# Listing the eight largest of every 512 adjacency columns, and gathering rows of x, beside the second layer's dense products

## The chip, the cores and the metric

The kernel runs on one core of a Trainium2 chip. The metric is the device time of one execution, in microseconds (us). The kernel before takes 2217.0 us, the median of two timed runs.

## The reference

Four graph layers work on the same node features x (4096 nodes by 128 features) and the same adjacency matrix adj (4096 by 4096, float32). About two in a thousand of its entries, and its diagonal, are nonzero. Each layer adds its result to x and normalizes every row.

```python
x = _layernorm(x + _L0_gnn_ref(x, adj, adj, L0_gnn_W, L0_gnn_a), axis=-1)
x = _layernorm(x + _L1_gnn_ref(x, adj, L1_gnn_W0, L1_gnn_b0, L1_gnn_W1, L1_gnn_b1), axis=-1)
x = _layernorm(x + _L2_gnn_ref(x, adj, L2_gnn_weight, L2_gnn_att_src, L2_gnn_att_dst, L2_gnn_bias), axis=-1)
x = _layernorm(x + _L3_gnn_ref(x, adj, L3_gnn_W_self, L3_gnn_W_neigh), axis=-1)
```

The second of them, where the change lies, is a Chebyshev convolution applied twice, with L = adj:

```python
def cheb_conv(x, L, W, b):
    Tx0 = x
    out = Tx0 @ W[0]
    Tx1 = L @ x
    out = out + Tx1 @ W[1]
    for k in range(2, W.shape[0]):
        Tx2 = 2.0 * (L @ Tx1) - Tx0
        out = out + Tx2 @ W[k]
        Tx0, Tx1 = (Tx1, Tx2)
    return out + b
h = jax.nn.elu(cheb_conv(x, L, W0, b0))
h = jax.nn.elu(cheb_conv(h, L, W1, b1))
```

## The kernel before

The adjacency matrix lies in device memory twice, as adj and as its transpose adjT, both cut by the host into blocks. A block of adjT is 512 by 512 and is loaded as one chunk of 1 MB: a tile of 128 partitions with four slices (k = 0 to 3) of 512 columns. The function `chunk` (line 128) takes the next tile of a pool `ld` of five such buffers and issues the load on SyncE's queue. The node features stay on chip, x by rows (32 tiles of 128 rows) and xT transposed.

The second layer needs four products with the adjacency matrix. They are reordered so that each is of a 4096-by-128 operand. The function `propagate` (line 656) makes one of them. Its outer loop runs over eight blocks of 512 output columns (ib); its inner loop runs over eight chunks (c), and each chunk gives four products of a 128x128 stationary operand with a 128x512 slice of the chunk, all summed in one bank of PSUM. At float32 each product is two matmul instructions in the profile, so a chunk is eight and a block 64. When a block is summed, `propagate` yields it and the caller works on it.

The four products are these. Operands in parentheses are the stationary ones.

- First propagation (x): the block is copied by ScalarE to t1T (line 679), transposed by TensorE and copied by VectorE to t1 (line 681). The order of its chunks is `finished`, the order in which the first layer completed the blocks of x, since it begins while the last blocks of x are still being normalized by VectorE (line 151).
- Second propagation (t1): VectorE makes t2T = 2 p - xT (line 686). TensorE multiplies xT, t1T and t2T by the three W0 matrices, for two halves of the hidden size (line 690). The function `elu` follows for each half: a relu on ScalarE (line 651), a minimum on VectorE (652), an exponential on ScalarE (653), and the sum on VectorE into hT (654). TensorE multiplies hT by twice the third W1 matrix (line 695), and VectorE copies the result to v (line 697).
- Third propagation (v): with hT and W1 added into the same sum (line 705), transposed and copied to w (line 711).
- A fourth product (w), at line 1126, runs in a part whose order is written out by hand, where the third layer's attention work starts on VectorE, ScalarE and GpSimd as blocks of x are completed.

Outside that last part the Tile framework orders the instructions of each engine by their readiness in a model of the program, and by program order among those that are ready. Each engine then runs its own list in order on the chip, and waits on semaphores. A buffer of a pool is taken again when all who use it are done, so a load of a chunk waits for every reader of the chunk that was in its buffer.

GpSimd has no work in the second layer. In the third layer it adds a bias to x (line 775) and makes a part of the products of attention weights and adjacency (lines 891, 892, 897 and 898).

Of the kernel before, what the change touches and what calls it, by code (L numbers as in the profile page):

```python
# [11 lines left out]
F32 = mybir.dt.float32  # L12
BF16 = mybir.dt.bfloat16
I32 = mybir.dt.int32
# [5 lines left out]
P = 128  # L20
IB = 512
TB = IB // P
# [11 lines left out]
def adj_resnorm_d4(ctx: ExitStack, tc: tile.TileContext, x_in, xT_in, adj, adjT, w0g, w0gT, a0, w1a, b1a,  # L34
# [7 lines left out]
    nc = tc.nc  # L42
    N, F = x_in.shape
    NT = N // P
    NB = N // IB
# [15 lines left out]
    x = state.tile([P, NT, F], F32, name="x")  # L61
# [63 lines left out]
    def chunk(pool, src, ib, c, name="chunk", pinned=False):  # L125

        t = pool.tile([P, TB, IB], F32, name=name)
        r = nc.sync.dma_start(t, src[ib, c])
        if pinned:
            tc.keep_in_program_order(r)  # L130
        return t

    def transpose4(pool, name, src, order=lambda r: r):

        p = pool.tile([P, TB, P], F32, name=name)
        for k in range(TB):
            order(nc.tensor.transpose(p[:, k, :], src(k), ident))  # L137
        return p
# [486 lines left out]
    def network(usual):  # L625

        with ExitStack() as whole:
# [3 lines left out]
            with ExitStack() as first, ExitStack() as l1h_pool:  # L631
                ps_acc, ps_tr, ps_mm = [first.enter_context(tc.tile_pool(name=n, bufs=2, space=PSUM, reuse_waits="tile"))
                                        for n in ("ps_acc", "ps_tr", "ps_mm")]
                if not usual:
                    layer0_general(ps_acc, ps_tr, ps_mm)
                    finished = list(range(NB))
                ld = enter(name="ld", bufs=5)
                if usual:
                    finished = layer0(ld, ps_acc, ps_tr, ps_mm)
                dv = state.tile([96, N], BF16, name="dv")  # L640
                l1w = l1h_pool.enter_context(tc.tile_pool(name="l1w", bufs=2, reuse_waits="tile"))
                l1h = l1h_pool.enter_context(tc.tile_pool(name="l1h", bufs=1, reuse_waits="tile"))
                W1A = l1h.tile([P, 3, HID], F32, name="W1A")
                nc.scalar.dma_start(W1A, w1a.rearrange("k p f -> p k f"))
                W1B = l1h.tile([P, 3 * HH, F], F32, name="W1B")
                nc.scalar.dma_start(W1B, w1b.rearrange("k (h p) f -> p (k h) f", p=P))

                def elu(dst, p, bias):
                    r = l1w.tile([P, IB], F32, name="elu_r")
                    n = l1w.tile([P, IB], F32, name="elu_n")  # L650
                    nc.scalar.activation(r, p, AF.Relu, bias=bias)
                    nc.vector.tensor_scalar(n, p, bias, 0.0, op0=ALU.add, op1=ALU.min)
                    nc.scalar.activation(n, n, AF.Exp)
                    nc.vector.scalar_tensor_tensor(dst, n, -1.0, r, op0=ALU.add, op1=ALU.add)

                def propagate(stationary, order=range(NB), beside=None):


                    for ib in range(NB):
                        p = ps_acc.tile([P, IB], F32, name="pacc")  # L660
                        for n, c in enumerate(order):
                            a = chunk(ld, adjT, ib, c)
                            for k in range(TB):
                                nc.tensor.matmul(p, stationary(c * TB + k), a[:, k, :], start=n == 0 and k == 0,  # L664
                                                 stop=n == NB - 1 and k == TB - 1)
                            if beside and n == 0:
                                beside(p, ib)
                        yield ib, slice(ib * IB, (ib + 1) * IB), p

                t1 = state.tile([P, NT, F], F32, name="t1", tag="yn")  # L670
                t1T = l1h.tile([P, N], F32, name="t1T")
                hT = l1h.tile([P, HH, N], F32, name="hT")
                wd = l1h.tile([P, HH, F], F32, name="wd")
                nc.vector.tensor_sub(wd, W1B[:, 0:HH, :], W1B[:, 2 * HH:3 * HH, :])
                w2x = l1h.tile([P, HH, F], F32, name="w2x")
                nc.vector.tensor_scalar_mul(w2x, W1B[:, 2 * HH:3 * HH, :], 2.0)

                for ib, blk, p in propagate(lambda jt: x[:, jt, :], finished):
                    nc.scalar.copy(t1T[:, blk], p)
                    q = transpose4(ps_tr, "ptr", lambda k: t1T[:, (ib * TB + k) * P:(ib * TB + k + 1) * P])  # L680
                    nc.vector.tensor_copy(t1[:, ib * TB:(ib + 1) * TB, :], q)

                v = state.tile([P, NT, F], F32, name="v")
                for ib, blk, p in propagate(lambda jt: t1[:, jt, :]):
                    t2T = l1w.tile([P, IB], F32, name="t2T")
                    nc.vector.scalar_tensor_tensor(t2T, p, 2.0, xT[:, blk], op0=ALU.mult, op1=ALU.subtract)
                    for hh in range(HH):
                        ph = ps_mm.tile([P, IB], F32, name="pmm")
                        for k, r in enumerate((xT[:, blk], t1T[:, blk], t2T)):
                            nc.tensor.matmul(ph, W1A[:, k, hh * P:(hh + 1) * P], r, start=k == 0, stop=k == 2)  # L690
                        elu(hT[:, hh, blk], ph, B1A[:, hh:hh + 1])
                    q = ps_tr.tile([P, TB, F], F32, name="ptr")
                    for k in range(TB):
                        for hh in range(HH):
                            nc.tensor.matmul(q[:, k, :], hT[:, hh, (ib * TB + k) * P:(ib * TB + k + 1) * P],
                                             w2x[:, hh, :], start=hh == 0, stop=hh == HH - 1)
                    nc.vector.tensor_copy(v[:, ib * TB:(ib + 1) * TB, :], q)


                w = state.tile([P, NT, F], F32, name="w", tag="yn")  # L700
                h0T = xT

                def times_w1(p, ib):
                    for hh in range(HH):
                        nc.tensor.matmul(p, W1B[:, HH + hh, :], hT[:, hh, ib * IB:(ib + 1) * IB], start=False, stop=False)

                for ib, blk, p in propagate(lambda jt: v[:, jt, :], beside=times_w1):
                    lvT = l1w.tile([P, IB], F32, name="t2T")
                    nc.scalar.copy(lvT, p)
                    q = transpose4(ps_tr, "ptr", lambda k: lvT[:, k * P:(k + 1) * P])  # L710
                    nc.vector.tensor_copy(w[:, ib * TB:(ib + 1) * TB, :], q)  # L711
                    ph = ps_mm.tile([P, IB], F32, name="pmm")
                    for hh in range(HH):
                        nc.tensor.matmul(ph, wd[:, hh, :], hT[:, hh, blk], start=hh == 0, stop=hh == HH - 1)
                    nc.scalar.copy(h0T[:, blk], ph)
# [328 lines left out]
            with tc.manual_schedule(engines={mybir.EngineType.PE, mybir.EngineType.DVE, mybir.EngineType.Activation,  # L1044
# [68 lines left out]
                for ib in range(NB):  # L1113
                    early = ib == 1
                    p = ps_nd.tile([P, IB], F32, name="num") if early else ps_p.tile([P, IB], F32, name="pp")
                    cuts = [0, 2, 4, 6, 8] if ib < 4 else [0, 1, 2, 4, 5, 6, 8] if ib < 6 else [0, 2, 4, 5, 6, 8]
                    for first, last in zip(cuts, cuts[1:]):
                        ks = [(c, k) for c in range(first, last) for k in range(TB)]
                        for n, (c, k) in enumerate(ks):
# [4 lines left out]
                            if k == 0:  # L1124
                                a = chunk(ld, adjT, ib, c)
# [55 lines left out]
            for _ in layer3_product(this.blocks):  # L1181
                pass

    network(True)
    with tc.If(nc.values_load(flag[0:1, 0:1], min_val=0, max_val=P) != 0):
        network(False)
# [32 lines left out]
```

## Time and profile before

| What | Value |
|---|---|
| Median of the two timed runs | 2217.0 us (2216.08 and 2217.92) |
| Span of the profiled execution, first to last instruction | 2213.3 us |
| TensorE matmul busy | 2139.9 us, 97% |
| VectorE busy | 1186.3 us, 54% |
| ScalarE busy | 562.4 us, 25% |
| GpSimd busy | 857.6 us, 39% |
| DMA moved | 528.18 MB, mean 239 GB/s |
| Granted TensorE clock, mean | 0.991 |

The profiled execution has no time of its own outside its span; the span stands 3.7 us below the median of the timed runs, and sums that are made from the profile are brought to the metric by that amount. PE is TensorE, PEld its load of stationary operands, DVE is VectorE, ACT is ScalarE, POOL is GpSimd, SP is SyncE, and a q behind a name is the engine's queue. The page cuts the span into 40 equal slices of 55 us each; a digit is the busy share in tenths. A line such as "L664 PE MATMUL pacc<-chunk,x" names the line of the kernel, the engine, the operation, the tile written and the tiles read. In a timeline the first number is the start in us, the second the time taken in us; what stands in brackets is the engine's idle time before and what ended it. In the list of waits the three numbers are total us, how often, and the longest.

### The profile page before, as it was taken

Reading aid. Unit: us, or ns where it says so; the run is one execution under the profiler, and the core shown is the slowest. Engines: PE = TensorE matmul, PEld = TensorE weight load, DVE = VectorE, ACT = ScalarE, POOL = GpSimd, SP = SyncE. Lnnn points to the kernel's source line nnn. Section 1 sums busy time; section 2 is a strip of 40 time slices with the busy share of each in tenths; the row PEclk is TensorE's granted clock in tenths of the full one; section 3 lists DMA queues with packets and bytes.
Section 4 is the critical chain, followed back from the end, with each engine's and each line's share of the span. In section 5 each row is a group of like instructions: output and inputs, shape, how many; then the busy total and the mean of one; then the engine's idle time right before and its main releaser. Section 6 shows DMA issues by size and latency. Waiting matters only on the chain. (4 is left out here: it accounts for less than half of the span.)

```text
span 2213.3 us, 22997 instructions
## 1 busy us (share of the span) xinstructions
PE 2139.9 (97%) x8644; PEld 850.8 (38%) x8644; DVE 1186.3 (54%) x1832; ACT 562.4 (25%) x1014; POOL 857.6 (39%) x539
## 2 busy tenths in 40 slices
PE   8999999999999999999999999979999899989997
PEld 3444454444444444444443333322222222333333
DVE  5655460000010110000026877899999999999995
ACT  6755100000000000000043223245333433332213
POOL 0000000000000000000004766698999999999980
PEclk9999999999999999999999999999999999999999
DMA  9886658888767677778876556525666566635545
GB/s 395 334 326 226 228 195 287 300 299 302 265 229 266 230 242 266 262 261 274 283 251 241 195 203 232 209 77 180 247 239 238 183 249 244 228 121 202 191 166 179
DMA packets 87145, 528.18 MB, mean 239 GB/s; under 512 B 9328, under 2 KB 15472, under 8 KB 25712
## 3 DMA queue, kind: packets, MB, share of 16 engines
q1 hardware_dynamic: 80288, 521.64, 66.8%
q10 hardware_dynamic: 6736, 4.98, 0.7%
q8 instruction: 70, 1.15, 0.2%
q14 instruction: 51, 0.42, 0.1%
HBM read 524.49 MB, written 2.10 MB: 238 GB/s over the span
## 5 line engine op out<-in xcount | busy, mean ns | idle before, releaser
L884 DVE SCALAR_TENSOR_TENSOR tau<-D,es,a 128x1024 f32<-128x1024 f32 (+1 forms) x640 | 646.4, 1058 | 44.0 <-ACT a L856 24.8
L892 POOL TENSOR_TENSOR tau<-tau,chunk 128x1024 f32<-128x1024 f32 x192 | 459.2, 2392 | 12.6 <-DVE tau L884 11.7
L775 POOL TENSOR_TENSOR x<-x,B2R 128x512 f32<-128x512 f32 x8 | 10.2, 1276 | 1145.5 <-PE px L137 1145.5
L908 PE MATMUL num<-tau,hc 128*32 128x512 f32 x2048 | 333.9, 606 | 15.0 <-POOL tau L892 9.0
L908 PE MATMUL den<-tau,cs 128*32 128x512 f32 x2048 | 343.6, 597 | 3.3 <-DVE tau L884 0.8
L999 PE MATMUL pp<-chunk,xT 128*128 128x512 f32 (+1 forms) x488 | 232.9, 607 | 0.0
L856 ACT ACTIVATE a<-chunk 128x1024 f32<-128x1024 f32 x160 | 164.2, 1026 | 254.8 <-DVE tau L890 195.1
L664 PE MATMUL pacc<-chunk,t 128*128 128x512 f32 x512 | 223.5, 592 | 0.0
L664 PE MATMUL pacc<-chunk,v 128*128 128x512 f32 x512 | 222.5, 592 | 0.0
L664 PE MATMUL pacc<-chunk,x 128*128 128x512 f32 x512 | 222.1, 592 | 0.0
L891 POOL TENSOR_TENSOR tau<-tau,chunk 128x320 f32<-128x320 f32 x192 | 167.7, 873 | 120.4 <-DVE tau L884 86.5
L1126 PE MATMUL pp<-chunk,w 128*128 128x512 f32 x448 | 204.3, 598 | 0.8 <-DVE oT L749 0.8
L379 PE MATMUL pacc<-chunk,hw 128*128 128x512 f32 x408 | 188.2, 606 | 2.4 <-DVE numT L407 1.7
L890 DVE TENSOR_TENSOR tau<-tau,a 128x704 f32<-128x704 f32 x186 | 163.1, 877 | 0.0
L898 POOL TENSOR_TENSOR tau<-tau,chunk 128x1024 f32<-128x1024 f32 x64 | 151.8, 2372 | 1.0
L908 PEld LDWEIGHTS num<-tau,hc 128*32 128x32 f32 x2048 | 62.4, 109 | 230.9 <-issue 127.8
L908 PEld LDWEIGHTS den<-tau,cs 128*32 128x32 f32 x2048 | 80.4, 110 | 177.0 <-issue 86.9
L664 PEld LDWEIGHTS pacc<-chunk,v 128*128 128x128 f32 x512 | 97.2, 190 | 122.0 <-issue 122.0
L664 PEld LDWEIGHTS pacc<-chunk,x 128*128 128x128 f32 x512 | 96.3, 190 | 115.8 <-issue 115.8
L664 PEld LDWEIGHTS pacc<-chunk,t 128*128 128x128 f32 x512 | 96.1, 190 | 115.3 <-issue 115.3
L999 PEld LDWEIGHTS pp<-chunk,xT 128*128 128x128 f32 x488 | 85.8, 190 | 133.1 <-issue 130.5
L711 DVE COPY w<-ptr 128x512 f32<-128x512 f32 x8 | 5.5, 691 | 241.5 <-PE ptr L137 241.5
(243 smaller groups left out, 1688.6 us busy)
## 6 DMA issues: line engine op xcount, KB each, us to landing
chunk<-in_adjT SPq DMA_DIRECT2D x386, 1024.0 KB, 4.9
chunk<-in_adj SPq DMA_DIRECT2D x80, 1024.0 KB, 5.0
chunk<-in_adj SPq DMA_DIRECT2D x32, 512.0 KB, 4.7
keep<-in_adjT SPq DMA_DIRECT2D x13, 1024.0 KB, 10.0
xT<-in_xT ACTq DMA_DIRECT2D x8, 256.0 KB, 6.6
out<-o ACTq DMA_DIRECT2D x7, 256.0 KB, 2.3
W1A<-in_w1a ACTq DMA_DIRECT2D x1, 384.0 KB, 5.4
W1B<-in_w1b ACTq DMA_DIRECT2D x1, 384.0 KB, 7.4
```

The source lines that it names most:

```text
L379: in_order(nc.tensor.matmul(p, hw[:, j * TB + k, :], a[:, k, :], start=first and k == 0, stop=last and k == TB - 1))
L664: nc.tensor.matmul(p, stationary(c * TB + k), a[:, k, :], start=n == 0 and k == 0, stop=n == NB - 1 and k == TB - 1)
L775: nc.gpsimd.tensor_tensor(x[:, tb, :], x[:, tb, :], B2R[:, None, :].to_broadcast([P, TB, F]), ALU.add)
L856: nc.scalar.activation(ap, a, AF.Copy, accum_out=deg[:, nt, self.mp:self.mp + 1])
L884: nc.vector.scalar_tensor_tensor(flat(tau[:, q:q + n]), flat(self.D[:, q:q + n]), es[:, nt, head:head + 1], ap, op0=ALU.max, op1=ALU.mult)
L890: nc.vector.tensor_tensor(t2[:, 0:OWN], t[:, 0:OWN], (a if only else ap)[:, 0:OWN], ALU.mult)
L891: nc.gpsimd.tensor_tensor(t2[:, OWN:WB], t[:, OWN:WB], a[:, OWN:WB], ALU.mult)
L892: nc.gpsimd.tensor_tensor(t2[:, WB:2 * WB], t[:, WB:2 * WB], a, ALU.mult)
L898: nc.gpsimd.tensor_tensor(tau2[:, 2:4, :], tau[:, 2:4, :], rep(a, 2), ALU.mult)
L908: nc.tensor.matmul(acc[32 * q:32 * q + 32, :], weights(nt, head, is_den), r[:, q, :], start=nt == 0, stop=nt == NT - 1)
L999: nc.tensor.matmul(p, y[:, c * TB + k, :], a[:, k, lo:lo + n], start=c == blocks[0] and k == 0, stop=end)
L1126: nc.tensor.matmul(p, w[:, c * TB + k, :], a[:, k, :], start=c == 0 and k == 0, stop=c == NB - 1 and k == TB - 1)
```

## The change

Each call of `propagate` can be given a function `seen`, which is called with every chunk. In the first propagation VectorE lists the chunks with an even c, in the second those with an odd c: for each of the four 128x512 slices of the chunk, the eight largest elements of each partition's 512 go to the tile `top`, and their positions to the tile `at`. Over both propagations every chunk is listed once. Nothing reads `top` or `at` later.

A table of 4096 rows in device memory receives a copy of x, by one DMA on ScalarE's queue. Then GpSimd issues 16 indirect DMAs for each of the eight blocks of the first propagation; each fetches 128 rows of 512 bytes from the table, one for each partition, by indices that stand in a column of the tile `rows`. They go to a tile `got` of four times 128 columns, of which there are two in turn. The indices are fixed numbers from a pattern (31 times the partition, plus the column), and nothing reads `got`. So the computation of the kernel's output is the same as before, dense products included.

```diff
-                def propagate(stationary, order=range(NB), beside=None):
+                def propagate(stationary, order=range(NB), beside=None, seen=None):
 
 
                     for ib in range(NB):
                         p = ps_acc.tile([P, IB], F32, name="pacc")
                         for n, c in enumerate(order):
                             a = chunk(ld, adjT, ib, c)
+                            if seen:
+                                seen(ib, c, a)
                             for k in range(TB):
                                 nc.tensor.matmul(p, stationary(c * TB + k), a[:, k, :], start=n == 0 and k == 0,
                                                  stop=n == NB - 1 and k == TB - 1)
...
-                for ib, blk, p in propagate(lambda jt: x[:, jt, :], finished):
+                if usual:
+                    top = l1h.tile([P, NT, NB, 8], F32, name="top")
+                    at = l1h.tile([P, NT, NB, 8], mybir.dt.uint16, name="at")
+                    rows = l1h.tile([P, 32], I32, name="rows")
+                    nc.gpsimd.iota(rows, pattern=[[1, 32]], base=0, channel_multiplier=31)
+                    table = whole.enter_context(tc.tile_pool(name="table", bufs=1, space=bass.MemoryType.DRAM)).tile([N, F], F32, name="table")
+                    nc.scalar.dma_start(table.rearrange("(t p) f -> p t f", p=P), x)
+
+                def largest(parity):
+                    def seen(ib, c, a):
+                        if c % 2 == parity:
+                            for k in range(TB):
+                                nc.vector.max(top[:, c * TB + k, ib, :], a[:, k, :])
+                                nc.vector.max_index(at[:, c * TB + k, ib, :], top[:, c * TB + k, ib, :], a[:, k, :])
+                    return seen if usual else None
+
+                for ib, blk, p in propagate(lambda jt: x[:, jt, :], finished, seen=largest(0)):
+                    if usual:
+                        for g in range(4):
+                            got = l1w.tile([P, 4, F], F32, name="got")
+                            for k in range(4):
+                                n = (ib * 16 + g * 4 + k) % 32
+                                nc.gpsimd.indirect_dma_start(got[:, k, :], None, table, bass.IndirectOffsetOnAxis(ap=rows[:, n:n + 1], axis=0))
                     nc.scalar.copy(t1T[:, blk], p)
                     q = transpose4(ps_tr, "ptr", lambda k: t1T[:, (ib * TB + k) * P:(ib * TB + k + 1) * P])
                     nc.vector.tensor_copy(t1[:, ib * TB:(ib + 1) * TB, :], q)
 
                 v = state.tile([P, NT, F], F32, name="v")
-                for ib, blk, p in propagate(lambda jt: t1[:, jt, :]):
+                for ib, blk, p in propagate(lambda jt: t1[:, jt, :], seen=largest(1)):
                     t2T = l1w.tile([P, IB], F32, name="t2T")
```

## The prediction

> **What bounds the kernel now.** I read the page first, for the span and for who is idle where. Slices 7 to 19 of its busy rows are the second layer: PE is at 9 throughout, VectorE at 0 or 1, GpSimd at 0.
>
> ```profile
> PE   8999999999999999999999999979999899989997
> DVE  5655460000010110000026877899999999999995
> POOL 0000000000000000000004766698999999999980
> PEclk9999999999999999999999999999999999999999
> DMA  9886658888767677778876556525666566635545
> ```
>
> Then I cut this part by the three propagations, by the first and last start of their matmuls (324.1 to 551.1 on x, 551.5 to 819.9 on t1, 825.5 to 1075.9 on v). The table of windows shows what room there is beside TensorE:
>
> ```profile
> core 0: us, PE busy (x) PEld busy (x) DVE busy (x) ACT busy (x) POOL busy (x), PEclk, DMA share, GB/s
> 337.00:551.00 214.00, 214.00 (x520) 95.45 (x519) 4.84 (x7) 4.10 (x7) 0.00 (x0) 1.00 0.88 300
> 551.00:825.00 274.00, 274.00 (x725) 128.32 (x724) 31.95 (x45) 21.29 (x32) 0.00 (x0) 1.00 0.73 251
> ```
>
> TensorE sets the pace in both: no idle, full clock. VectorE has 209 us free in the first and 242 us in the second. GpSimd is empty, and its timeline has nothing between 1.3 us and 1115.66 us:
>
> ```profile
> 1.01 0.29 POOL masks.py:199 TENSOR_SCALAR_AFFINE_SELECT ident<-ident 128x128 f32<-128x128 f32 x1
> 1115.66 1.27 POOL L775 TENSOR_TENSOR x<-x,B2R 128x512 f32<-128x512 f32 x1 [1114.36 <-PE px L137]
> ```
>
> Third, VectorE's timeline in the second propagation, which shows the only VectorE operations there for which TensorE waits soon:
>
> ```profile
> 614.08 0.69 DVE L686 SCALAR_TENSOR_TENSOR t2T<-pacc,xT 128x512 f32<-128x512 f32 x1 [22.49 <-PE pacc L664]
> 617.44 0.75 DVE L652 TENSOR_SCALAR elu_n<-pmm,B1A 128x512 f32<-128x512 f32 x1 [2.66 <-ACT elu_r L651]
> 618.88 0.69 DVE L654 SCALAR_TENSOR_TENSOR hT<-elu_n,elu_r 128x512 f32<-128x512 f32 x1 [0.70 <-ACT elu_n L653]
> ```
>
> Last, the waits of SyncE's queue, which issues the loads, and the landing of the chunk loads from 337 to 551 us: a load waits for TensorE to give back one of five buffers, and then lands quickly.
>
> ```profile
> SPq L128 <- PE pacc L664: 670.4, 191, 8.4
> ```
>
> ```profile
> DMA to landing us min/median/max: 4.6/4.8/5.7
> ```
>
> **The pace and the slack of a chunk.** In the first propagation blocks end every 27.94 us (the t1T copies stand at 384.08, 412.03, 439.97), so a chunk is used every 3.49 us, or 3.43 us of matmuls. A load starts when the chunk five before it is released, and TensorE begins on its data four chunks later, 13.7 us; it lands after 4.8 us. So a chunk lies ready about 8.9 us before it is needed, and VectorE may hold a buffer up to 8.9 us beyond TensorE before anything waits. In the second propagation blocks take 34.41 us (t2T at 579.68, 614.08, 648.49).
>
> [...]
>
> **The change part by part.** Nothing is removed, and none of the results is read later. So it can only cost; the question is what is hidden.
>
> *Listing.* The first propagation lists even chunks, the second odd ones: 8 blocks x 4 chunks x 4 tiles = 128 tiles in each. One tile: the maxima 0.69 us (nearest row, 128x512 f32), loading the eight values 0.16 us (128x4 operations of this trace take 0.16), a hand-over 0.04 us (dependent 128x4 operations follow at 0.20), the search 0.69 us, less 0.08 us in which independent operations overlap (300.48 to 301.06 for one of 0.66). That is 1.50 us. Lower bound 1.2 (two passes at 0.60, no load), upper 2.03[...]. Per block 16 x 1.50 = 24.0 us, plus 0.7 in the first propagation = 24.7 of 27.94, and plus 4.3 (0.69, twice 0.75 and 0.69, 0.69) in the second = 28.3 of 34.41. VectorE keeps up. Even chunks that follow each other in the order of the first propagation let it fall behind for a few us, which the 8.9 us cover. Cost: 0. If that cover were gone, each us above 27.94 per block would show on TensorE.
>
> *What queues behind a listing.* VectorE runs in order. At a block's end in the first propagation only the copy of t1 waits, needed one propagation later: 0. In the second, t2T is ready 0.83 us before TensorE takes it (ends 580.37, used 581.20), and hT 0.74 us before (584.92 + 0.69 = 585.61, used 586.35). One listing operation in front, 0.69, just fits; two do not, and ScalarE's and VectorE's steps alternate. Bounds 0 and 3 us a block; I take 0.8: 8 x 0.8 = 6 us. Before 335 us VectorE also finishes layer 0, with TensorE behind it in order; listing operations in its gaps cost 0 to 6 us, I take 2.
>
> *The table.* ScalarE's queue issues one DMA of x, 4096 rows of 512 B, once x is done at 335.4 us. The next thing due from ScalarE after its copies of xT is t1T at 356.14, so a block on its queue of under 1 us (the like-shaped load of x took 0.84 us to issue, 13.0 us to land) is hidden. A 512 B packet takes 27 ns and an 8192 B packet 309 ns in the packets of this trace, so the table holds each of 16 engines for 256 x 27 ns = 6.9 us.
>
> *The gathers.* 128 DMAs of 128 rows: 8 rows per engine each, 1024 x 27 ns = 27.6 us per engine in all. They wait only for the table, the index tile and a buffer, not for the block. A chunk takes an engine 8 x 309 ns = 2.47 us, so the first propagation needs 64 x 2.47 = 158 us; with 6.9 and 27.6 it is 193 of about 228. The busy share 0.88 is higher than this since one packet in ten takes over 0.6 us; but between 150 and 160 us the same queue ran at 419 GB/s, against 300 needed. Cost 0, by 8.9 us of early landing. GpSimd's own time per gather is in no row.[...] I take 2: 256 us, done near 600 us, long before 1115.66. Cost: 0.
>
> Sum: 2213.3 + 6 + 2 = 2221.3 us of span. The span lies 3.7 us under the median of the two timed runs, 2217.0; so 2225.
>
> **Rivals.**
> 1. *VectorE becomes the bound, slower.* At 2.03 us a tile the first propagation needs 32.5 + 0.7 = 33.2 us a block, 5.3 above TensorE's, 42 us in eight, less 9 of buffers = 33. The second needs 36.8 against 34.41, 19 us, and some 8 us as its chain finds VectorE always busy. With the 2 above, 62: 2279. It passes 2% (44 us) from about 1.97 us a tile. For it: the search has no row, and two passes leave 14% of VectorE in the first propagation.[...]
> 2. *GpSimd is late, slower.* The first product of the third layer that needs it starts at 1176.24; from 337 us that allows (1176 - 337) / 128 = 6.6 us a gather.[...] at 7 us about 2280. For it: unmeasured, one index a partition.[...]
> 3. *The loads starve.* If a gathered row took 200 ns instead of 27, the engines would owe 128 x 2.47 + 205 + 7 = 528 us in the 496 us of both propagations: 32 us, with the chain's 8 about 2257. Against: the 512 B packets of this trace.
> 4. *The listings are dropped or fully hidden*: 2217. Nothing reads them, but nothing in the code takes them out.
>
> **How the numbers follow.** Forecast 0.58, rival 1 0.18, rival 2 0.12, rival 3 0.07, rival 4 0.05. A change within 2%, 44 us, is about what a measurement of this kernel can tell from none. Slower by more takes rivals 1 and 2 and a part of 3 and of the forecast's upper end: 0.36. Faster by over 2% has no mechanism, as nothing is removed: 0.01. Within: 0.63. The range runs from 2215 (all hidden, spread of the timed runs) to 2285 (rival 1 entire, rival 2 up to 7 us); it leaves out most of rival 2 and little else. The likeliest case alone: 2216 to 2236.
>
> **What would show it.** Right: blocks of the first propagation still end every 27.9 us; each listing instruction near 0.69 us; VectorE near 0.87 busy at 337 to 551; GpSimd's last gather before 700 us; TensorE's new idle time in the second propagation put down to t2T or hT. Wrong: chunk loads that wait for VectorE's search and not for TensorE, blocks longer than 28 us (rival 1); line 775 or 891 starting after 1180 (rival 2); landings over 9 us and matmuls that wait for chunk loads (rival 3).

## Result, and the profile after

The changed kernel took 2349.7 us (two runs, 2348.4 and 2351.1) against 2217.0: a ratio of 1.0605, 95% interval 1.0574 to 1.0636. It is slower by 6%. The profiled execution took 2351.06 us, with a span of 2349.0.

That is not the whole result. Run again on four chips, this same kernel took 2216.0 us (12 runs), 2215.8 (10 runs) and 2218.1 (one run) on three of them, and 2348.2 (one run) on the fourth. So the experiments have two questions: what takes the 133 us where they are lost, and why only there.

The busy rows of the page after, each digit a slice of 58.7 us, show where the time went:

```profile
PE   8999998317999999999999999997999999989997
DVE  5654685105776767100002577789999999999995
POOL 0000005770000000000000466669999999999990
PEclk9999999558999999999999999999999999999999
DMA  9886666336886766787777655653666566635445
```

TensorE was at 9 throughout before. Now it falls to 8, 3, 1 and 7 in slices 6 to 9, counted from 0, and GpSimd, empty there before, is at 5, 7 and 7 in slices 6 to 8. DMA falls to 3 in slices 7 and 8: the transfers were not crowded, they were missing. The list of TensorE's instructions on the accumulator gives the three propagations (first and last start):

```profile
L666 PE MATMUL pacc<-chunk,x x512: 589/592/1222, 323.6 to 685.2; 128*128 128x512 f32 x171
L666 PE MATMUL pacc<-chunk,t x512: 592/592/595, 685.7 to 955.5; 128*128 128x512 f32 x171
L666 PE MATMUL pacc<-chunk,v x512: 592/592/595, 961.1 to 1211.8; 128*128 128x512 f32 x171
```

From the first matmul on x to the first on t it is 362.1 us, before 227.4: 134.7 more. From there to the first on v it is 275.4 us, before 274.0. So 134.7 of the 135.7 us by which the span grew lie in the first propagation. The table of windows, cut there by what GpSimd does (gathers from 364.0 to 523.6 us):

```profile
core 0: us, PE busy (x) PEld busy (x) DVE busy (x) ACT busy (x) POOL busy (x), PEclk, DMA share, GB/s
324.00:365.00 41.00, 40.17 (x114) 18.66 (x113) 33.40 (x105) 2.94 (x6) 0.97 (x1) 1.00 0.88 316
365.00:410.00 45.00, 38.22 (x85) 16.77 (x84) 23.15 (x55) 0.58 (x1) 33.20 (x37) 0.92 0.61 212
410.00:525.00 115.00, 28.09 (x28) 7.38 (x27) 15.35 (x36) 0.00 (x0) 86.77 (x92) 0.51 0.34 99
525.00:560.00 35.00, 15.89 (x34) 7.49 (x35) 10.92 (x25) 0.58 (x1) 0.00 (x0) 0.65 0.48 167
560.00:700.00 140.00, 140.00 (x342) 62.47 (x341) 104.85 (x245) 2.93 (x5) 0.00 (x0) 1.00 0.87 301
```

TensorE has its full pace up to the gathers, starts 28 matmuls in 115 us while they run, and has its full pace again soon after. The new groups of the page (count, busy us, mean ns, idle time before and what ended it):

```profile
L702 POOL DMA_INDIRECT got<-table,rows x128 | 120.9, 945 | 402.1 <-DVE top L692 362.6
L692 DVE MAX8 top<-chunk 128x8 f32<-128x512 f32 x256 | 163.3, 679 | 155.8 <-DMA chunk<-in_adjT 116.0
L693 DVE FIND_INDEX8 at<-top,chunk 128x8 uint16<-128x512 f32 x256 | 172.1, 684 | 0.0
```

Each pass of the listing has the length that was forecast. VectorE waits for loads. The other way round it is rare: SyncE's queue waits three times for VectorE's search, 11.0 us in all, each time before 365 us, where TensorE stays busy, and never during the stall. TensorE's timeline during the gathers (start, length, and in brackets the idle time before it with its releaser):

```profile
444.00 1.01 PE L666 MATMUL pacc<-chunk,x 128*128 128x512 f32 x1 [2.36 <-issue]
446.80 1.01 PE L666 MATMUL pacc<-chunk,x 128*128 128x512 f32 x1 [1.79 <-issue]
...
484.60 2.08 PE L666 MATMUL pacc<-chunk,x 128*128 128x512 f32 x2 [3.18 <-DMA chunk<-in_adjT]
544.11 1.11 PE L137 MATMUL ptr<-ident,t1T 128*128 128x128 f32 x4 [57.43 <-ACT t1T L703]
```

The matmuls of a chunk start 2.1 to 4.2 us apart, six of the eight alone and two together, and most gaps are put to "issue", that is to nothing the profile shows. Chunks come about 22.4 us apart, 8 x 2.8. The last two lines show a second effect: the block's last matmul ends at 486.68, and the copy of t1T that waits for it starts at 543.47 (ScalarE's timeline), 56.8 us later, with ScalarE idle all the time. In the kernel before, the 64 matmuls of a block took 27.63 us, one every 0.43 us, and the copy started within a microsecond of their end; the two lines of before stand last here:

```profile
543.47 0.58 ACT L703 COPY t1T<-pacc 128x512 f32<-128x512 f32 x1 [153.53 <-remote]
```

```profile
413.16 27.63 PE L664 MATMUL pacc<-chunk,x 128*128 128x512 f32 x64
439.97 0.59 ACT L679 COPY t1T<-pacc 128x512 f32<-128x512 f32 x1 [27.36 <-PE pacc L664]
```

So TensorE's instructions run late and its completions are seen late, and both stop about 20 us after the gathers do. The granted clock of 0.51 goes with it, but does not make the gaps: a matmul of 1.01 us in place of 0.59 explains 0.4 us of 2.8, and from 365 to 390 us TensorE already stands idle for 5.8 us at a clock of 0.98.

### The profile page after: what moved, and what is told of

Its sections match the earlier page's. It is cut to its first block, busy times and chain, and to the rows that moved or that the text cites. A ratio compares the mean times of both kernels' runs of the same rounds, so it can differ in the third digit from the quotient of the medians.

```text
span 2349.0 us, 23964 instructions
## 1 busy us (share of the span) xinstructions
PE 2163.6 (92%) x8644; PEld 855.7 (36%) x8644; DVE 1508.1 (64%) x2600; ACT 561.7 (24%) x1014; POOL 978.7 (42%) x668
## 3 DMA queue, kind: packets, MB, share of 16 engines
q0 software_dynamic: 4096, 8.40, 1.3%
## 5 line engine op out<-in xcount | busy, mean ns | idle before, releaser
L908 DVE SCALAR_TENSOR_TENSOR tau<-D,es,a 128x1024 f32<-128x1024 f32 (+1 forms) x640 | 646.4, 1058 | 43.0 <-ACT a L880 24.5
L666 PE MATMUL pacc<-chunk,x 128*128 128x512 f32 x512 | 243.0, 627 | 49.5 <-issue 41.3
L702 POOL DMA_INDIRECT got<-table,rows x128 | 120.9, 945 | 402.1 <-DVE top L692 362.6
L692 DVE MAX8 top<-chunk 128x8 f32<-128x512 f32 x256 | 163.3, 679 | 155.8 <-DMA chunk<-in_adjT 116.0
L693 DVE FIND_INDEX8 at<-top,chunk 128x8 uint16<-128x512 f32 x256 | 172.1, 684 | 0.0
```

The source lines that it names most:

```text
L693: nc.vector.max_index(at[:, c * TB + k, ib, :], top[:, c * TB + k, ib, :], a[:, k, :])
L908: nc.vector.scalar_tensor_tensor(flat(tau[:, q:q + n]), flat(self.D[:, q:q + n]), es[:, nt, head:head + 1], ap, op0=ALU.max, op1=ALU.mult)
```

## Experiments

The numbers of chips only tell them apart; the chip of the two recorded runs is not known. "Kernel before" is the median beside it on the same chip. A time that has no count of runs beside it is one run.

### One half of the change alone, and other ways to issue the transfers (chip 1, kernel before 2213.8)

Listing alone:

```
-  rows = ...; nc.gpsimd.iota(rows, ...); table = ...; nc.scalar.dma_start(table, x)
-  nc.gpsimd.indirect_dma_start(got[:, k, :], None, table, ...)        # 128 of them
```

> The table and the 128 gathers are left out, the listing stays. Theory A (the stall from 390 to 540 us comes with the gathers; the listing is hidden): about 2219 us, that is before plus the 2 us by which the second and third propagation grew in the changed kernel, and the first propagation ends near 551 us as before. Theory B (the listing holds the chunk buffers and so starves TensorE): about 2340 us, the first propagation again near 685 us.

Measured: 2215.15 us (20 runs), ratio 1.0006, interval 0.9999 to 1.0012. The listing is hidden on this chip.

Gathers alone:

```
-  top = ...; at = ...
-  return seen if usual else None
+  return None
```

> The listing is left out, the table and the 128 gathers stay. Theory A: the stall is there with its whole size, about 2347 us, loads of chunks again 22.4 us apart while the gathers run. Theory B: about 2217 us. If the two only together make the stall (both readers of a chunk and the gathers), about 2217 us here and about 2219 us with the listing alone.

Measured: 2214.2. During the gathers a load still starts every 3.49 us (46 between 366.1 and 523.0 us), at 350 GB/s. I read this as "the gathers are not enough", and the experiments that followed built on it. That was wrong, as shown below.

Plain transfers of 128 rows, issued by GpSimd or by ScalarE:

```
-  nc.gpsimd.indirect_dma_start(got[:, k, :], None, table, bass.IndirectOffsetOnAxis(ap=rows[:, n:n + 1], axis=0))
+  nc.gpsimd.dma_start(got[:, k, :], table[n * P:(n + 1) * P, :])      # or nc.scalar.dma_start
```

> Listing and table stay; the 128 indirect gathers become 128 plain copies of 128 rows of the table, issued by GpSimd too, same bytes, same rows of 512 B, no indices. Theory A1[...]: a stall again, 2320 to 2350 us, while GpSimd issues. Theory A2 (the indirect form does it[...]): about 2219 us.

> As the one before, but ScalarE's queue issues the 128 plain copies. Theory A1[...]: no stall of 22 us a chunk, about 2219 us, up to 2230 where ScalarE's copies of t1T wait behind the issues. Theory A3 (the traffic of 16,384 rows of 512 B itself, whoever issues it): 2300 us or more.

Measured: 2215.9 from GpSimd and 2263.3 from ScalarE. The second loses 49 us in an ordinary way. On ScalarE's timeline the first three t1T copies stand behind transfers: they start at 371.24 us after 20 of them, at 413.54 after 75, and at 457.75 after all 128. Issuing these holds ScalarE's queue for 0.45 us each (median), 58 us in all, and in between the queue waits for a free `got` buffer: they take from 358.3 to 457.3 us. From the waits of TensorE in that kernel (total us, times, longest):

```profile
PE ptr L137 <- ACT t1T L701: 40.7, 3, 14.9
```

GpSimd waits for the same buffers, but no work for which TensorE waits stands behind it. Its list of instructions on `got` in the kernel with plain transfers from GpSimd, with the waits ahead of them:

```profile
L700 POOL DMA_DIRECT2D got<-table x128: 534/534/707, 364.5 to 498.6; - x128
...
  DMA got<-table: 64.3, 27
```

### Variants of what seemed to be an interaction (chip 13, kernel before 2214.5)

Two GpSimd additions on a scratch tile after each gather, all of them kept in the order of the program:

```
+  for _ in range(2):
+      nc.gpsimd.tensor_tensor(pad, pad, pad, ALU.add)
```

> Listing, table and gathers all stay; GpSimd adds a scratch tile to itself twice after each gather, some 2.5 us, so that a gather starts every 3.8 us and not every 1.25 us. Theory C1 (TensorE's completions pile up only while gathers come close together beside the listing): the stall is gone, 2215 to 2225 us. Theory C2 (each gather beside the listing costs TensorE about 1 us, 135 us for 128): the cost stays, 2340 us, spread over the first two propagations.

A quarter of each row gathered:

```
-  got[:, k, :], None, table
+  got[:, k, 0:32], None, table.rearrange("n (q f) -> (n q) f", q=4)
```

> As the changed kernel, but each gathered row is 128 bytes and not 512:[...] a quarter of the bytes. If the descriptors or the indirect instruction do it: 2350 us as with whole rows. If the bytes written into the on-chip memory do it: well below, 2215 to 2260 us.

Two plain reductions in place of the listing:

```
-  nc.vector.max(...); nc.vector.max_index(...)
+  nc.vector.tensor_reduce(top[...], a[:, k, :], AX.X, ALU.max); nc.vector.tensor_reduce(..., ALU.add)
```

> Gathers and table stay. In place of the eight largest and their positions VectorE makes the maximum and the sum of each 128x512 slice: two passes of about 0.69 us over the same chunks at the same places, but no pair of dependent instructions. Theory D1 (any VectorE work of this density beside indirect gathers does it): 2340 to 2350 us. Theory D2 (it is particular to the listing instructions, with their short load and the semaphore between): about 2217 us.

The listing reads xT and not the chunk:

```
-  nc.vector.max(top[...], a[:, k, :])                # and max_index
+  nc.vector.max(top[...], xT[:, c * IB:(c + 1) * IB])
```

> Gathers and table stay; the listing instructions are as many, but read columns of xT and not the chunk, so that they neither hold a chunk's buffer nor add VectorE to what a load of a chunk waits for. If the stall comes from chunks held by two readers: about 2217 us. If it comes from the listing instructions running beside the gathers, whatever they read: 2330 us or more.

Measured: 2227.1, 2215.7, 2215.8 and 2231.8, none with a stall in the first propagation. Since the unedited kernel was not among them, they say nothing on what the stall needs. Two of them, the additions and the listing on xT, cost time for reasons that can be read. With xT, the listing needs no load and keeps VectorE busy without a gap from 365 to 560 us and beyond (its first instruction starts at 319.5, its last at 665.4); the first t2T of the second propagation queues behind it. From TensorE's waits:

```profile
PE pmm L714 <- DVE t2T L710: 13.9, 1, 13.9
```

With the additions, the loss (288.0 us for 274.0) lies in the second propagation. From the groups of VectorE and of GpSimd there:

```profile
L654 DVE SCALAR_TENSOR_TENSOR hT<-elu_n,elu_r 128x512 f32<-128x512 f32 x14 | 22.4, 1603 | 0.7 <-ACT elu_n L653 0.7
...
L714 DVE SCALAR_TENSOR_TENSOR t2T<-pacc,xT 128x512 f32<-128x512 f32 x7 | 4.8, 688 | 1.2 <-PE pacc L666 1.0
...
L706 POOL TENSOR_TENSOR pad<-pad 128x512 f32<-128x512 f32 x256 | 270.8, 1058 | 12.2
```

The same operation that makes hT takes 675 ns in the changed kernel without the additions (on chip 9). Beside GpSimd's additions it takes 1603 ns, and TensorE waits 11.1 us for it, most of the 14.0. The operation that makes t2T, with one operand in PSUM, keeps its 688 ns. The trace does not say why one slows and the other does not.

### The kernel again, and three more variants (chip 9, kernel before 2214.0)

The changed kernel, nothing edited:

> The changed kernel once more, nothing edited, on whatever chip this call gets. Theory together (search instructions on chunk and whole-row gathers, 1.25 us apart, hold back TensorE's completions): the first propagation is as long as before, about 361 us, the kernel at 2345 to 2355 in every round. Rival chance (the stall is a matter of that chip or of how two streams happened to fall together, so that the near variants which kept 2214 to 2231 say nothing on their edits): the rounds scatter between 2217 and 2350, or all lie near 2217.

Measured: 2216.0 us (12 runs, 2213.9 to 2217.0), ratio 1.0009, interval 1.0000 to 1.0018. No stall in any run. The profile of one of them, windows and gathers:

```profile
410.00:525.00 115.00, 115.00 (x283) 51.39 (x283) 84.38 (x197) 2.93 (x5) 81.40 (x87) 1.00 0.98 349
```

```profile
L702 POOL DMA_INDIRECT got<-table,rows x128: 938/944/1129, 362.6 to 530.0; - x128
...
DMA to landing us min/median/max: 3.3/5.4/6.7
```

The instructions are the same, the gathers run at nearly the same time and take the same 944 ns each, but TensorE has no gap, and 349 GB/s are moved in that window instead of 99. The theory that listing and gathers hold TensorE back wherever they overlap fell here, and with it every reading of the variants above as a cure.

The gathers written at the block ends of the third propagation, where nothing is listed:

```
   for ib, blk, p in propagate(lambda jt: v[:, jt, :], beside=times_w1):
+      (the 16 gathers of the block)
```

> All of the change's work, but the 16 gathers of a block are issued at the block ends of the third propagation, where nothing is listed, instead of the first. Theory together: listing and gathers no longer overlap, no stall, 2214 to 2219 as with the listing alone. Rival gathers with chunk loads (the gathers hold back any propagation that runs close to its loads): the stall moves to the third propagation, its 250 us become about 385, the kernel near 2350. In both the gathers stay 1.25 us apart.

Measured: 2215.8 (20 runs), but the edit did not do what it was for. The gathers still stood from 362.4 to 526.3 us, beside the listing:

```profile
L731 POOL DMA_INDIRECT got<-table,rows x128: 938/944/1129, 362.4 to 526.3; - x128
```

GpSimd's queue holds nothing else there, and a gather waits for no block, so where it is written in the loop does not set when it is issued.

No positions (`max_index` left out), and half of the matmuls of the first propagation (`range(0, TB, 2)`), which leaves out half of its sum:

> The positions are left out: VectorE finds the eight largest (MAX8) and looks up no index; the gathers stay. If the look-up (MATCH_VALUE_LOAD with FIND_INDEX8) is the part of the listing that meets the gathers: no stall, 2214 to 2219. If any search instruction that reads chunk does, or if VectorE's reading of chunk alone does: half as many instructions, a stall of half the size or all of it, 2280 to 2350.

> The first propagation multiplies only the even 128-row tiles of each 512-row chunk (2 matmuls a chunk for 4; half of the sum is left out); loads, listing and gathers stay. Outside the gathers the loads bound it at about 3.0 us a chunk or less. If the stall has a price for each TensorE instruction that signals (22.4 us a chunk over four matmuls with their weight loads), chunks come 11 us apart while the gathers run, and the first propagation lasts some 225 to 300 us. If it has a price for each chunk load or each listed tile, 22 us as before and about 340 to 360 us. If the stall needs a full TensorE queue, it is gone, and the first propagation takes about 200 us.

Measured: 2218.8 and 2179.0, no stall in either, which on this chip tells nothing of the stall. The second has the loads as its bound: the first propagation takes 193.9 us, 3.0 us a chunk, at 399 GB/s between 410 and 525 us.

### On which chips, and is the listing needed

The rest were repeats of two kernels: the changed kernel and the gathers alone. First on chip 4 (kernel before 2213.6):

> The changed kernel again, nothing edited. Theory chip (the stall belongs to the chip, or the session, of the recorded run): 2214 to 2218 here in every round, unless this call gets such a chip, and then about 2350 in every round. Theory chance (it comes and goes from run to run): some rounds near 2217, some near 2350.

> Gathers without the listing, on the chip of the run beside it. If the changed kernel stalls on this chip: 2214 here says that listing and gathers are needed together, 2350 that the gathers are enough. If it does not stall there: 2214 to 2217, and nothing told.

Measured: 2215.8 (10 runs, 2214.5 to 2219.3; ratio 1.0010, interval 1.0000 to 1.0020) and 2215.5. No stall.

The changed kernel on chip 7 and on chip 5:

> The changed kernel, nothing edited, one look on a chip not used for it yet. Theory chip or session (of the recorded run alone): 2214 to 2218. If stalling chips are common, about 2350.

> The changed kernel, nothing edited, one more look. Theory chip or session (of the recorded run alone): 2214 to 2218. If stalling chips are common, about 2350.

Measured: 2218.1 on chip 7 (kernel before 2214.1), 2348.2 on chip 5 (kernel before 2216.4). The windows of these two, chip 7 ahead:

```profile
410.00:525.00 115.00, 115.00 (x284) 51.60 (x283) 84.08 (x197) 2.93 (x5) 79.59 (x85) 1.00 0.97 349
```

```profile
410.00:525.00 115.00, 31.32 (x32) 8.50 (x31) 16.30 (x39) 0.00 (x0) 84.94 (x91) 0.51 0.33 98
```

The stall came back in the size of the recorded runs (first propagation 360.8 us, there 362.1). The kernel before ran at its usual time on this chip.

The gathers alone, on chip 9 and on chip 0:

> Gathers without the listing. On the chip where the changed kernel takes 2348: if the gathers alone hold TensorE's completions back, about 2348 again; if the listing is needed beside them, 2214 to 2218. On any other chip 2214 to 2218, which tells nothing new.

> Gathers without the listing once more. On the chip where the changed kernel takes 2348: about 2348 if the gathers alone are enough, 2214 to 2218 if the listing is needed beside them. On any other chip 2214 to 2218, which tells nothing new.

Measured: 2214.6 on chip 9 (kernel before 2214.5), and 2341.6 on chip 0 (kernel before 2213.6). On chip 0, the first propagation and the gathers, from the lists of instructions:

```profile
L666 PE MATMUL pacc<-chunk,x x512: 589/592/1222, 322.7 to 676.7; 128*128 128x512 f32 x171
```

```profile
L700 POOL DMA_INDIRECT got<-table,rows x128: 939/946/1131, 355.9 to 516.1; - x128
```

TensorE's timeline has the same two signs, with VectorE almost empty (0.69 us busy in the 115 us from 410 to 525):

```profile
440.50 1.01 PE L666 MATMUL pacc<-chunk,x 128*128 128x512 f32 x1 [1.58 <-issue]
443.30 1.01 PE L666 MATMUL pacc<-chunk,x 128*128 128x512 f32 x1 [1.79 <-issue]
...
506.10 2.08 PE L666 MATMUL pacc<-chunk,x 128*128 128x512 f32 x2 [2.90 <-DMA chunk<-in_adjT]
536.61 1.12 PE L137 MATMUL ptr<-ident,t1T 128*128 128x128 f32 x4 [28.43 <-ACT t1T L701]
```

The first propagation lasts 354.4 us (322.7 to the first matmul on t1 at 677.1) with gathers and no listing at all; before it is 227.4. That answers the first question: the listing is not needed, and the table with its indirect gathers is enough, on a chip that stalls. It costs 128.0 us there, against 131.8 with the listing on chip 5 and 132.7 in the recorded runs. Whether the listing adds the few us between them was not measured on one chip, and the listing alone was not run where the stall occurs.

It also tells something of the earlier chips. The gathers alone did not stall on chip 1, and two of the kernels of chip 13 kept all 128 gathers unchanged and did not stall. So neither chip was one that stalled at the time, and none of the variants run there can have cured anything.

**What is shown, and what stays open.** Shown: the loss is in the first propagation; it begins 20 to 28 us after the first gather and ends about 19 us after the last, in all three traces; the gathers cause it without the listing; the same kernel has it in the recorded runs and on chip 5, and not in 23 runs on chips 4, 7 and 9.

Open: what differs between these chips, which was the second question. The two stalling experiments are one run on each chip, so a state of a chip at that time cannot be told from the chip itself. Chip 9 was met at two times, once with the changed kernel and once with the gathers alone, and did not stall at either.

Open too is the path by which GpSimd's gathers reach TensorE: the trace names none ("issue", "remote"). The traces do show one more thing that goes with the stall. All these runs were recorded by the profiler, and where there is no stall it has 2019 to 2048 records of the landings of the 128 indirect gathers, 16 for each; in full on chips 1 and 4. In the recorded run it has 209, on chip 5 192 and on chip 0 219, although the packets of the gathers are all there, 4096 in the recorded run and on chip 5. This is why those traces give no time to landing. They are missing before TensorE's first gap, at 384 us, too: from 370 to 380 us there are 13, on chip 9 122. With so many records missing, "issue" and "remote" are weak words, and a rival stays untested: that the stall lies in the recording of so many events, and would not come without it. No run was made without recording. Whether plain transfers from GpSimd, or shorter rows, would avoid the stall was not tried on a chip that has it.

## Why the prediction was wrong, step by step

**The step that failed** is the gathers, "Cost: 0". It priced them by what they take from two resources, GpSimd's time and the DMA engines', and both estimates were safe. GpSimd issues one every 1.25 us (0.945 busy), below the 2 taken, and is done at 523.6 us, before the 700 named. The DMA room was there: on chip 9 the window 337 to 551 us has a share of 0.98 at 351 GB/s, the loads land after 6.5 us (median, 360 to 540 us) in place of 4.8, within the 8.9 of cover, and TensorE has no gap. What the sum lacked is a term for the gathers' effect on TensorE itself. Where the stall occurs it measures 134.7 / 128 = 1.05 us a gather in the recorded run, and 127.0 / 128 = 0.99 us on chip 0 with the gathers alone. No row of the trace of before could have shown it, since GpSimd did nothing there; but the text took "in no row" as a doubt on GpSimd's own duration alone, and gave no chance to an effect on the engine that sets the pace. So the range, to 2285, was too short. How the effect comes about stays open, as said above; on a chip without the stall the same step would have come true, which would have been luck with the chip.

**The steps that held or were only mis-sized:**
- *Listing*, 1.50 us a tile: 1.25 (two tiles in 2.51 us), as maxima 0.68, load of the values 0.07, search 0.68, with more overlap than taken. The search runs at the pace of the maxima. VectorE was 0.77 busy from 337 to 551 us on chip 9, for 0.87 forecast. Cost 0 agrees with the listing alone on chip 1, ratio 1.0006.
- *What queues behind a listing*, 6 us: 0.7 on chip 9, where the second propagation takes 274.7 us for 274.0. In the recorded profile TensorE's idle time in it is put to t2T, as forecast, but it is 0.6 us.
- *Layer 0's end*, 2 us: no cost is seen. The first matmul on x starts at 322.7 us on chip 9, before at 324.1.
- *The table*: 0.41 us of ScalarE's queue, landed after 24.8 us on chip 9; nothing on TensorE's path waits for it. Right.
- *A gather's own time*, 2 us of GpSimd, was the author's estimate, from no row of a trace: measured 0.945 us for 128 indices, and 5.4 us from issue to landing (median, chip 9, beside transfers of 349 GB/s in all).
- A reading: the 419 GB/s given for 150 to 160 us is the rate of the later part of that stretch; its mean is 388, still above the 349 to 351 that were moved on chip 9.

Where there is no stall the reasoning holds and its size is four times too large: 8 us forecast, 2.0 measured on chip 9 (2216.0 against 2213.97). The profiled run there is the fastest of the 12, 2213.88, so its trace cannot tell where the 2.0 lie.

**The rivals.** VectorE as the bound: no, at 1.25 us a tile, where the 2.03 was the author's estimate; only the listing on xT kept it busy throughout. GpSimd late: no, its gathers end at 523.6 us. Loads starve: the closest in looks, since some matmuls wait for chunks; but the share of the DMA engines fell to 0.34, and SyncE's queue, which issues the loads, itself stood waiting (135.4 us in eight waits from 365 to 545 us, put to nothing that the profile names and none of them to VectorE). Everything hidden: right to 0.2% on three chips. None of them was the mechanism of the loss.

## What to carry to other kernels

Work on an idle engine is priced by its own time and its bandwidth only as long as it leaves the pacing engine alone; 128 indirect gathers that delay nobody by either measure went with a loss of 128 to 133 us in the runs on some chips, and of 4 us or less, listing included, on others. When an experiment takes a loss away, run the unedited kernel beside it on the same chip: here eight variants ran without a stall on chips that did not have it. When a stall is put to nothing that the profile shows, count the profile's own records before trusting its words. For work that waits on nothing in the loop, its place in the text does not set when it is issued, so look at the start times before reading a move.

## What the hardware showed that I had not expected

- While indirect gathers ran under the profiler, TensorE on some chips started matmuls 2.1 to 4.2 us apart in place of 0.43, and a completion reached ScalarE up to 57 us late; VectorE's listing instructions kept their 0.68 us. Nine in ten records of the gathers' landings are missing from those traces.
- An indirect gather of 128 rows of 512 B holds GpSimd 0.945 us and goes out every 1.25 us; a plain transfer of as many rows holds it 0.534 us.
- VectorE's operation that makes hT, with both operands in SBUF, took 1603 ns in place of 675 beside GpSimd additions of 1058 ns; the one that makes t2T, with one operand in PSUM, took 688 ns beside them and 689 without.
